# A depool, cross-projection and channel-mix chain: two projections as plain float32 matmuls, and the first loads in another order

## The chip, the cores and the metric

The kernel runs on one core of a Trainium2 chip. The metric is the device time of one execution in microseconds. Five engines work side by side, each through its own queue of instructions in order: TensorE (PE, matmuls and transposes through the array, results into PSUM), VectorE (DVE), ScalarE (ACT), GpSimd (POOL) and SyncE (SP, which here only issues transfers). PEld is TensorE's loading of the stationary operand.

## What is computed

There are 16 batches of 512 rows with 512 channels (`x`), a context of 512 rows with 1024 channels per batch, and a table of patch lengths. Cut to what matters, for each batch:

```python
n1   = layernorm(x)
h    = rmsnorm(n1) * g_res @ W_in + b_in               # "a"
hp   = rmsnorm(ctx) * g_init                           # first 512 channels are used
s[t] = ADEC * s[t-1] + BCOEF * hp[t]                   # scan over the 512 rows
x    = x + h + s[plug]                                 # plug: rows from a running sum of patch lengths
n2   = layernorm(x);  prev = n2 shifted down by one row
xk   = mu_k * n2 + (1 - mu_k) * prev                   # xr the same with mu_r
k    = square(relu(xk @ W_k.T))                        # "k"
x    = x + sigmoid(xr @ W_r.T) * (k @ W_v.T)           # "r", "v"
```

All of it is float32, with four projections of 512x512x512 per batch: a, k, r and v.

## The kernel before

**Matmuls in three passes.** A float32 operand is split into a high part (rounded to the matmul's reduced float32 type, `F32R`) and a low part (the rest). A projection of 512 columns and one block of 128 rows is twelve matmuls of 128x128x512: high by high, high by low weights, low by high weights, each over four pieces of the 512 channels (`QW`, line 595). The split takes, for each of four pieces, a cast on ScalarE (high) and a subtraction on VectorE or GpSimd (low). This holds for the weights (`hi_w`, `lo_w`, lines 574 and 577, into `wha`, `wla` and so on), for x (`split_x`, line 638, into `xh`), for the mixes (`mix`, line 860, into `m`) and for k (`k_mm`, line 904, into `ka`). A plain float32 matmul is used only for `pm` (line 1114, a mean of the weights under g_res, from which the correction of the weights, line 1124, is worked out) and for the scan's carry `pc` in the first two batches (line 749).

**One batch.** Context rows are squared and summed on ScalarE (`sq`), scaled and scanned over four interleaved row blocks on VectorE (`scan_u`), carried over the partitions by one matmul (`scan`), updated and written to a scratch tensor in memory (`dr`). Meanwhile x is turned by TensorE for the batches in `BY_PE` (`turn_x`, results `tx`; other batches load a transposed copy, `raw`), split, and projected (`a_first` for batch 0, `a_mm` for the others, results `pa`). The bias is added to x either by VectorE or GpSimd (batches in `BIAS_ADD`) or by an accumulating transfer issued by GpSimd (line 703). `a_end` (line 809) adds the projection, scaled by the row's inverse deviation, to x on VectorE. Four gathers from `dr` accumulate into x (`gather`, line 816, indirect transfers of GpSimd; for b < `NLATE` after the row ends). `norm2` normalizes (result `y`, on VectorE for batches in `Y_DVE`, else on ScalarE), `transp` turns y (`tr`), `mix` makes the two shifted mixes, and k, r and v follow, then stores. `a_first` and `k_first` go through the channel pieces in the outer loop and the four row blocks in the inner one, so all four results end together; `a_mm` finishes one row block after the other.

**Order.** Every piece of work is registered with a cost, its reads and writes, and a due time (`Plan.add`). `Plan.order` (line 119) plays the engines and transfers through and fixes each engine's queue by earliest deadline among what is ready and has a free buffer. Due times of matmuls come from a list, `slot` (line 1069): first what `START` names (line 446: x0, a0, a1, x1, x2, a2, k0, t0), from `T0` on; then for each batch i what `PERIOD` names (line 319: projection i+1, k of i), r and v of i, with the transposes of i+1 among them. `SHIFT` moves the deadlines of a stage, `ONLY` (line 392) pins the subtractions and bias adds of a stage to VectorE (0) or GpSimd (1), `ON_ACT` and `KR_DVE` choose engines for row statistics and squares. All queues are fixed when the program is built. `WARM` (line 419) puts dummy matmuls of 128x128 ahead of some groups, `HEAT` dummy matmuls of 512 columns at the very start.

**First loads.** Line 1094 on: the small constants, W_in (`load_w("a")`, two halves, tiles `wsa`), the scan's constants, the four row blocks of x0; then line 1134 on: g_init broadcast, the four context blocks of batch 0, b_in broadcast. Deadlines `at` fix this order in SyncE's queue.

Of the kernel before, what the change touches and what calls it, by code (L numbers as in the profile page):

```python
# [26 lines left out]
NC = 4  # L27
# [262 lines left out]
class InOrder:  # L290
# [27 lines left out]
PASS = 0.935  # L318
PERIOD = lambda i: (("a", i + 1), ("k", i))
TAT = {0: (0, 1), 2: (2, 3)}  # L320
TAT_OF = {0: {0: (0, 1, 2, 3)}, 1: {0: (0, 1, 2, 3)}, 2: {0: (0, 1, 2, 3)}}
# [3 lines left out]
HEAT = 8  # L325
SHIFT = {
    ("a", 0): 2.1,
    ("gather", 0): 23.8,
    ("k", 0): 2.0,
    ("load", 0): -10.1,  # L330
    ("mix_k", 0): 5.2,
    ("mix_r", 0): -10.7,
    ("norm2", 0): -17.9,
    ("plugs", 0): -30.6,
    ("rv", 0): 1.3,
    ("scan", 0): -7.2,
    ("sq", 0): -19.5,
    ("stat1", 0): -7.7,
    ("store", 0): 1.6,
    ("wk", 0): -5.2,  # L340
    ("wv", 0): -6.2,
    ("a", 1): 10.4,
    ("bias", 1): 2.6,
    ("gather", 1): 3.0,
    ("k", 1): 4.0,
    ("mix_k", 1): -1.5,
    ("mix_r", 1): -3.9,
    ("norm2", 1): -3.6,
    ("plugs", 1): 0.3,
    ("rv", 1): 12.6,  # L350
    ("split_x", 1): -7.5,
    ("sq", 1): -9.3,
    ("stat1", 1): 0.2,
    ("a", 2): 1.0,
    ("bias", 2): 53.6,
    ("gather", 2): -18.5,
    ("load", 2): 5.1,
    ("mix_k", 2): 1.2,
    ("mix_r", 2): 4.1,
    ("norm2", 2): 6.6,  # L360
    ("rv", 2): -0.4,
    ("scan", 2): 0.4,
    ("split_x", 2): -5.3,
    ("sq", 2): 30.1,
    ("stat1", 2): -1.6,
    ("store", 2): -50.4,
    ("a", 3): 8.2,
    ("bias", 3): -12.0,
    ("gather", 3): -1.8,
    ("k", 3): -3.2,  # L370
    ("load", 3): -3.1,
    ("mix_r", 3): -1.7,
    ("norm2", 3): 10.1,
    ("split_x", 3): 9.0,
    ("sq", 3): 2.7,
    ("stat1", 3): -16.2,
    ("store", 3): 9.3,
    ("a", 4): 13.9,
    ("bias", 4): -18.4,
    ("gather", 4): 11.9,  # L380
    ("k", 4): 4.9,
    ("load", 4): 16.5,
    ("mix_k", 4): 0.0,
    ("mix_r", 4): -47.3,
    ("norm2", 4): -4.5,
    ("plugs", 4): 4.7,
    ("rv", 4): -2.0,
    ("split_x", 4): -0.3,
    ("sq", 4): 2.2,
    ("stat1", 4): 2.5,  # L390
    ("store", 4): -10.4,
}
ONLY = {
    ("rv", 0): 0,
    ("k", 2): 0,
    ("wr", 0): 0,
    ("k", 3): 1,
    ("mix_r", 0): 0,
    ("split_x", 3): 0,
    ("bias", 1): 0,  # L400
    ("wk", 0): 1,
    ("mix_r", 2): 0,
    ("rv", 3): 0,
    ("mix_k", 0): 1,
    ("wv", 0): 0,
    ("wv", 1): 0,
    ("mix_k", 3): 1,
    ("rv", 2): 0,
    ("wk", 3): 1,
    ("bias", 3): 0,  # L410
    ("wr", 2): 0,
    ("wr", 3): 1,
    ("mix_k", 2): 1,
    ("split_x", 2): 0,
    ("wv", 2): 0,
}
BIAS_ADD = (0, 1)
BY_PE = (0, 1, 2)
WARM = {
    ("k", 1, 0): 1,  # L420
    ("x", 2): 32,
    ("a", 3, 0): 15,
    ("r", 0, 0): 14,
    ("a", 2, 1): 7,
    ("a", 0, 0): 29,
    ("x", 0): 1,
    ("v", 0, 0): 10,
    ("x", 1): 1,
}
TIE = 5.0  # L430
KR_DVE = (1, 3, 4, 5, 10, 11, 15)
# [4 lines left out]
RAW_IN = {2: ("op", "raw")}  # L436
CX_IN = {}
NLATE = 4
NWHOLE = 2
Y_DVE = (0, 1, 2, 3)  # L440
LEAD = 12.0
HI_DVE = False
U_DVE = True
LOADS = ["raw2"]
B_DUE, P_DUE = 3.31, 83.3
START = [("x", 0), ("a", 0), ("a", 1), ("x", 1), ("x", 2), ("a", 2), ("k", 0), ("t", 0)]
T0 = 14.3
ON_ACT = (0, 1, 3, 4, 5, 6, 9, 10, 11, 13, 15)
# [3 lines left out]
def block_kernel(  # L452
# [88 lines left out]
    LO = ((DVE, 0.61), (POOL, 1.26))  # L541

# [94 lines left out]

    def split_x(b, c):
        if b in BY_PE:
            n, t = f"xh{b}_{c}", f"tx{b}_{c}"  # L640
            add((ACT, 0.52), lambda e: e.copy(S[n][:, 0], S[t]), K(t, *J), K(n, 0), new={n: OP}, early=40)
            add((DVE, 0.6), lambda e: e.tensor_tensor(S[n][:, 1], S[t], S[n][:, 0].bitcast(F32), ALU.subtract),
                K(t, *J) + K(n, 0), K(n, 1))
            return
# [99 lines left out]
    def scan(b):  # L744
# [3 lines left out]
        if b < NWHOLE:  # L748
            add((PE, 1.12), carry, K(f"cx{b}_{NJ - 1}") + K("consts"), K(f"pc{b}"),
                new={f"pc{b}": PST if b == 0 else PS}, lead=LEAD if b > 1 else 0.0)  # L750
        else:
# [10 lines left out]
            def carry3(e):  # L762
# [4 lines left out]
                new={f"pc{b}": PS}, lead=LEAD if b > 1 else 0.0)  # L767
# [13 lines left out]

    def a_mm(b, j, due, kind=PS):
        n = f"pa{b}_{j}"
        sl = slice(j * P, (j + 1) * P)
        new = warm(("a", b, j), {n: kind}, due)
        for k, (q, w) in enumerate(QW):
# [8 lines left out]
    def a_first():  # L795

        ns = [f"pa0_{j}" for j in J]
        new = warm(("a", 0, 0), {n: TRP for n in ns}, due["a", 0, 0])
        for k, (q, w) in enumerate(QW):
# [274 lines left out]
    for what, b in START:  # L1074
        if b < NB and (what != "x" or b in BY_PE):
            for j in J:
                slot((what, b, j), 0.43 if what in "tx" else 3 * PASS)
# [16 lines left out]
    add((SP, 0.5), lambda e: e.dma_start(small_in, small_d), (), K("cols") + K("msk") + K("tri"), moves=0.45, at=-9.5)  # L1094
    load_w("a", at=-9)
    add((SP, 0.5), lambda e: e.dma_start(consts, consts_d), (), K("consts"), moves=0.4, at=-8.5)
    for j in J:
        load_x0(j, -8)
# [32 lines left out]
    def row(src, dst, k, at):  # L1131
        add((SP, 0.5), lambda e: e.dma_start(dst, src.unsqueeze(0).broadcast_to([P, D])), (), K(k), moves=0.8, at=at)

    row(ginit[0:D], g_bc, "g_bc", -6.4)
    for j in J:
        load_ctx(0, j, at=-6)
# [14 lines left out]
    def prepare_batch(b):  # L1151
# [50 lines left out]
        if b == 0:  # L1202
            a_first()
# [128 lines left out]
```

## Time and profile before

Times of three runs: 812.93, 815.05 and 817.34 us, median 815.05. One execution was profiled:

| | us |
|---|---|
| the profiled execution's own time | 813.32 |
| its span, first to last instruction | 811.2 |
| first matmul of projection a, batch 0 | 18.66 |
| first row ends of batch 0 on VectorE | 34.93 |
| first transposes of y, batch 0 | 54.96 |
| first matmul of k, batch 0 | 70.04 |
| first matmul of r, batch 0 (dummies ahead of it from 82.54) | 83.29 |
| matmul busy time, whole span | 789.8 |
| VectorE busy time, 0 to 82.5 us | 71.4 |
| ScalarE busy time, 0 to 82.5 us | 53.4 |
| GpSimd busy time, 0 to 82.5 us | 41.4 |

The time of an execution is a little more than its span. Busy times count overlapping ends of pipelined matmuls once. All instructions but a few are recorded under one line of a helper (L300), so groups are told apart by the names of their tiles: `pa`, `pk`, `pr`, `pw` are the results of a, k, r, v; `tx` and `tr` the transposes of x and y; `pm` and `pc` the two float32 matmuls; `wsa` the unsplit weights, `wha` and `wla` their parts, and likewise with k, r and v.

### The profile page before, as it was taken

To read this page: it belongs to the slowest core of one execution; us is meant where nothing else is said; L and a number is where in the kernel's file an instruction comes from. 1 tells how busy PE (TensorE), PEld (TensorE's weight loads), DVE (VectorE), ACT (ScalarE), POOL (GpSimd) and SP (SyncE) were. 2 spreads that over 40 slices of the span, in tenths; PEclk is the share of its full clock that TensorE was granted. 3 is DMA by queue.
4 is the path that set the end of the run, shared out by engine and by line. 5 is a ranking of instruction groups with operands and counts; after the bars stand their busy time and mean duration, and the time that the engine had idled before them with its cause. 6 is when DMAs were issued, how large, how long until landed. Compare 5 with 4: busy or idle time off the path is not lost.

```text
span 811.2 us, 11218 instructions
## 1 busy us (share of the span) xinstructions
PE 789.8 (97%) x3627; PEld 624.8 (77%) x3627; DVE 616.2 (76%) x1323; ACT 486.7 (60%) x950; POOL 449.8 (55%) x374
## 2 busy tenths in 40 slices
PE   7998999999999999999999999999999999999997
PEld 4776777877777887878787887888778787888885
DVE  6899799989789497686968779685876869784622
ACT  5937496555484566757455775646666564655640
POOL 2843676464675465763647566565665647571300
PEclk9999999999999999999999999999999999999999
DMA  9857486884784773847668392866559477350001
GB/s 321 271 96 263 101 235 175 280 216 131 157 232 131 181 232 74 241 166 198 156 140 242 74 268 107 218 198 184 135 130 246 136 173 216 66 141 2 27 27 52
DMA packets 52554, 134.69 MB, mean 166 GB/s; under 512 B 4752, under 2 KB 5264, under 8 KB 50576
## 3 DMA queue, kind: packets, MB, share of 16 engines
q1 hardware_dynamic: 35744, 102.39, 36.9%
q0 software_dynamic: 16608, 31.46, 23.0%
q8 instruction: 28, 0.46, 0.2%
q14 instruction: 30, 0.25, 0.1%
q10 hardware_dynamic: 144, 0.13, 0.0%
HBM read 85.73 MB, written 33.55 MB: 147 GB/s over the span
## 4 chain that ended last, share of the span: by engine, by line
PE 62%; DVE 12%; DMA 9%; POOL 6%; issue 5%; ACT 4%; SPq 0%; POOLq 0%; DVEq 0%; ACTq 0%
PE pk L300 19%; PE pr L300 15%; PE pw L300 14%; PE pa L300 11%; DMA x<-dr,plug 6%; DVE cx L300 4%; PE tr L300 3%; DVE pv L300 2%; DVE x L300 2%; POOL m L300 2%; DMA dr<-cx 2%; POOL x L300 2%; ACT pv L300 2%; PE pc L300 1%; ACT junk L300 1%
## 5 line engine op out<-in xcount | busy, mean ns | idle before, releaser
L300 POOL TENSOR_TENSOR m<-pv,m 128x512 fp32r<-128x512 f32 x79 | 117.1, 1492 | 54.6 <-ACT m L300 23.3
L300 PE MATMUL pr<-whr,m 128*128 128x512 f32 x512 | 141.7, 400 | 0.8 <-ACT sg L300 0.8
L300 PE MATMUL pa<-wha,xh 128*128 128x512 f32 x512 | 136.0, 400 | 5.6 <-DVE x L300 2.7
L300 POOL DMA_INDIRECT x<-dr,plug x64 | 109.8, 1715 | 55.8 <-DMA dr<-cx 16.8
L300 PE MATMUL pw<-whv,ka 128*128 128x512 f32 x512 | 138.9, 397 | 0.6 <-ACT sg L300 0.6
L300 PE MATMUL pk<-m,whk 128*128 128x512 f32 x512 | 134.4, 397 | 2.5 <-DVE x L300 2.1
L300 ACT ACTIVATE pv<-tr,om 128x384 f32<-128x384 f32 (+1 forms) x256 | 100.5, 488 | 57.7 <-PE tr L300 44.6
L300 PEld LDWEIGHTS pa<-wha,xh 128*128 128x128 f32 x512 | 94.8, 188 | 33.4 <-DVE x L300 7.3
L300 PEld LDWEIGHTS pk<-m,whk 128*128 128x128 f32 x512 | 95.2, 188 | 27.9 <-DVE x L300 2.9
L300 PEld LDWEIGHTS pw<-whv,ka 128*128 128x128 f32 x512 | 95.6, 188 | 24.1 <-ACT sg L300 1.8
L300 PEld LDWEIGHTS pr<-whr,m 128*128 128x128 f32 x512 | 94.0, 188 | 22.3 <-ACT sg L300 1.2
L300 DVE SCALAR_TENSOR_TENSOR pv<-tr,small,pv 128x511 f32<-128x511 f32 x128 | 95.0, 743 | 11.3 <-ACT pv L300 9.2
L300 ACT ACTIVATE y<-x,r 128x512 f32<-128x512 f32 x48 | 39.0, 816 | 97.3 <-DVE r L300 95.3
L300 DVE TENSOR_TENSOR sg<-pw,sg 128x512 f32<-128x512 f32 (+1 forms) x65 | 44.0, 678 | 55.6 <-PE pw L300 55.4
L300 POOL TENSOR_TENSOR xh<-raw,xh 128x512 fp32r<-128x512 f32 x48 | 64.4, 1348 | 39.1 <-ACT xh L300 22.6
L300 POOL TENSOR_TENSOR x<-x,sg 128x512 f32<-128x512 f32 x14 | 19.3, 1378 | 113.9 <-DVE sg L300 94.5
L300 ACT CAST m<-pv 128x512 fp32r<-128x512 f32 x128 | 73.2, 628 | 15.1 <-DVE pv L300 12.2
L300 ACT ACTIVATE junk<-cx 128x1024 bf16<-128x1024 f32 x64 | 67.9, 1061 | 12.3 <-DMA cx<-cx 11.6
L300 ACT ACTIVATE sg<-pr 128x512 f32<-128x512 f32 x64 | 38.1, 598 | 56.5 <-PE pr L300 47.3
L300 PE MATMUL pa<-wla,xh 128*128 128x512 f32 x256 | 70.4, 398 | 0.3 <-POOL wla L300 0.3
L300 PE MATMUL pw<-wlv,ka 128*128 128x512 f32 x256 | 70.7, 398 | 0.0
L300 PE MATMUL pr<-wlr,m 128*128 128x512 f32 x256 | 70.3, 396 | 0.0
(116 smaller groups left out, 1300.7 us busy)
## 6 DMA issues: line engine op xcount, KB each, us to landing
cx<-cx SPq DMA_DIRECT2D x64, 512.0 KB, 6.2
dr<-cx SPq DMA_DIRECT2D x64, 256.0 KB, 3.4
out<-x SPq DMA_DIRECT2D x31, 512.0 KB, 2.8
x<-x SPq DMA_DIRECT2D x15, 1024.0 KB, 4.9
x<-bc POOLq DMA_DIRECT2D x14, 1024.0 KB, 8.1
raw<-xT SPq DMA_DIRECT2D x26, 512.0 KB, 7.5
wsa<-winT SPq DMA_DIRECT2D x2, 512.0 KB, 4.4
x<-x SPq DMA_DIRECT2D x4, 256.0 KB, 7.0
```

The lines of the kernel that those rows point to most:

```text
L300: r = self._tc.keep_in_program_order(op(*args, **kwargs))
```

## The change

Projection a of batches 0 and 1 (`A_WHOLE`) takes four float32 matmuls per row block, on the unsplit weights `wsa` and on an unsplit copy `xt` of the transposed x, which ScalarE or VectorE copies from PSUM. The split weights of a are still made, for the batches from 2 on. Batch 0's projection goes row block by row block (`ROWS_FIRST`). The projection of batch 2 and the transposes of x2 leave `START`, so they come in the period of batch 1, ahead of its k and behind r and v of batch 0. The first loads follow a list, `FIRST`: context first, then W_in and x0. `WARM` is empty. Engine choices change: y of batches 0 and 1 on ScalarE, the low parts of wr and wv on GpSimd, batch 0's bias on GpSimd, batch 1's bias by transfer and batch 2's on GpSimd, other squares and statistics; batch 3 gathers ahead of its row ends (`NLATE`). All deadlines shift (`SHIFT`), and with them each engine's order. The carry's `LEAD` gets a second constant for late batches.

```diff
+WHOLE = 0.86
-TAT = {0: (0, 1), 2: (2, 3)}
-TAT_OF = {0: {0: (0, 1, 2, 3)}, 1: {0: (0, 1, 2, 3)}, 2: {0: (0, 1, 2, 3)}}
+TAT = {2: (0, 1, 2, 3)}
+TAT_OF = {0: {0: (0, 1, 2, 3)}, 1: {3: (0, 1), 5: (2, 3)}, 2: {2: (0, 1), 4: (2, 3)}, 3: {0: (0, 1), 2: (2, 3)}, 4: {0: (0, 1), 2: (2, 3)}}
-HEAT = 8
+HEAT = 9
...
-    ("split_x", 2): 0,
-    ("wv", 2): 0,
+    ("wr", 1): 1,
+    ("rv", 1): 0,
+    ("bias", 1): 1,
+    ("split_x", 2): 1,
 }
-BIAS_ADD = (0, 1)
+BIAS_ADD = (0, 2)
 BY_PE = (0, 1, 2)
-WARM = {
-    ("k", 1, 0): 1,
-    ("x", 2): 32,
-    ("a", 3, 0): 15,
-    ("r", 0, 0): 14,
-    ("a", 2, 1): 7,
-    ("a", 0, 0): 29,
-    ("x", 0): 1,
-    ("v", 0, 0): 10,
-    ("x", 1): 1,
-}
+WARM = {}
...
-RAW_IN = {2: ("op", "raw")}
-CX_IN = {}
-NLATE = 4
+RAW_IN = {0: ("op", "raw"), 1: ("op", "raw"), 3: ("raw", "op")}
+CX_IN = {1: ("cx", "op"), 2: ("op", "cx"), 3: ("op", "cx")}
+NLATE = 3
 NWHOLE = 2
-Y_DVE = (0, 1, 2, 3)
+FIRST = ["cx0_3", "small", "cx0_0", "consts", "g", "cx0_1", "cx0_2", "wa", "x0", "b"]
+ROWS_FIRST = True
+Y_DVE = (2, 3)
+A_WHOLE = (0, 1)
...
-LOADS = ["raw2"]
-B_DUE, P_DUE = 3.31, 83.3
-START = [("x", 0), ("a", 0), ("a", 1), ("x", 1), ("x", 2), ("a", 2), ("k", 0), ("t", 0)]
-T0 = 14.3
+LOADS = ["cx1", "raw2", "raw1"]
+B_DUE, P_DUE = 1.31, 0.91
+START = [("x", 0), ("a", 0), ("x", 1), ("a", 1), ("k", 0), ("t", 0)]
+T0 = 1.55
...
+    CP = ((ACT, 0.52), (DVE, 0.6))
...
+    def xt(b, c):
+
+        return S[f"xt{b}_{c // 2}" if b in BY_PE else f"raw{b}_{c // 2}"][:, c % 2]
+
     def split_x(b, c):
+        if b in A_WHOLE:
+            if b in BY_PE:
+                n, t = f"xt{b}_{c // 2}", f"tx{b}_{c}"
+                add(CP, lambda e: copy(e, S[n][:, c % 2], S[t]), K(t, *J) + (K(n, "a") if c % 2 else []),
+                    K(n, c % 2) + ([] if c % 2 else K(n, "a")), new=None if c % 2 else {n: STAGE}, early=40)
+            return
...
     def a_mm(b, j, due, kind=PS):
         n = f"pa{b}_{j}"
         sl = slice(j * P, (j + 1) * P)
         new = warm(("a", b, j), {n: kind}, due)
+        if b in A_WHOLE:
+            for c in range(NC):
+                add((PE, WHOLE), lambda e, c=c: e.matmul(S[n], xt(b, c)[:, sl], st("a", c), start=(c == 0), stop=(c == NC - 1)),
+                    XT(b, c) + K(f"wsa{c // 2}", c % 2), K(n), new=None if c else new, due=due + c * WHOLE, early=AHEAD)
+            return
...
-                slot((what, b, j), 0.43 if what in "tx" else 3 * PASS)
+                slot((what, b, j), 0.43 if what in "tx" else 4 * WHOLE if what == "a" and b in A_WHOLE else 3 * PASS)
...
+    for k, what in enumerate(FIRST):
+        load_first(what, 0.05 * k - 9.5)
...
-        if b == 0:
+        if b == 0 and not ROWS_FIRST:
             a_first()
         for j in J:
-            if b:
-                a_mm(b, j, due["a", b, j], PST if b == 1 else PS)
+            if b or ROWS_FIRST:
+                a_mm(b, j, due["a", b, j], PST if b < 2 else PS)
             a_end(b, j)
```

## The prediction

> **What bounds the kernel now.** I read the busy table first, then the busy tenths, the stretches of the first 83 us, TensorE's timeline and last SyncE's queue. The first view gives share of the span and instruction counts.
>
> ```profile
> PE 789.8 (97%) x3627; PEld 624.8 (77%) x3627; DVE 616.2 (76%) x1323; ACT 486.7 (60%) x950; POOL 449.8 (55%) x374
> ...
> PE   7998999999999999999999999999999999999997
> ```
>
> TensorE is the bound nearly everywhere; the waits that release it after 82.5 us add up to 4.3 us in all. So the span is: the moment at which the first k is through, plus the rest of TensorE's work, plus a tail (its last matmul ends near 806.3 us, the span at 811.2 us). The stretches show where the beginning differs (columns: stretch, length, then busy time and count of PE, PEld, DVE, ACT, POOL, granted clock, DMA share, GB/s).
>
> ```profile
> 15.00:16.00 1.00, 1.00 (x12) 1.00 (x11) 0.97 (x4) 1.00 (x3) 0.07 (x1) 0.50 1.04 412
> ...
> 20.00:40.00 20.00, 18.05 (x113) 14.10 (x114) 17.63 (x39) 18.30 (x44) 16.99 (x15) 1.00 0.81 277
> 40.00:60.00 20.00, 18.40 (x93) 14.68 (x92) 19.21 (x51) 6.42 (x15) 10.28 (x11) 1.00 0.63 101
> 60.00:80.00 20.00, 17.14 (x80) 12.16 (x79) 19.76 (x44) 16.37 (x34) 6.94 (x6) 1.00 0.77 264
> ```
>
> From 40 to 80 us VectorE is busy 19 to 20 us of 20, TensorE is not: up to the first k the bound is VectorE and the chain through it. TensorE's timeline (start, us, engine, line, op, result<-operands, count, and in brackets what it waited for) gives the prices.
>
> ```profile
> 5.29 3.67 PE L300 MATMUL pm<-wsa,gmean 128*128 128x512 f32 x8
> 9.52 2.58 PE L300 MATMUL tx<-consts,x 128*128 128x128 f32 x16 [0.56 <-DMA x<-x]
> ...
> 14.78 3.27 PE L300 MATMUL pa<-ones 128*128 128x128 f16 x29 [0.50 <-DVE pf L300]
> 18.66 1.20 PE L300 MATMUL pa<-wha,xh 128*128 128x512 f32 x4 [0.61 <-ACT wha L300]
> ...
> 33.30 1.91 PE L300 MATMUL tx<-consts,x 128*128 128x128 f32 x16
> ...
> 70.04 2.46 PE L300 MATMUL pk<-m,whk 128*128 128x512 f32 x8 [0.74 <-DVE x L300]
> ...
> 82.54 0.94 PE L300 MATMUL pr<-ones 128*128 128x128 f16 x14
> 83.29 1.17 PE L300 MATMUL pr<-whr,m 128*128 128x512 f32 x4
> 84.30 1.09 PE L300 MATMUL pr<-wlr,m 128*128 128x512 f32 x4
> 85.23 2.03 PE L300 MATMUL pr<-whr,m 128*128 128x512 f32 x8
> 87.10 1.10 PE L300 MATMUL pr<-wlr,m 128*128 128x512 f32 x4
> ```
>
> The last rows: eight split matmuls from 85.23 to 87.10, 0.234 us each, so 2.80 us for one row block's twelve and 11.2 us for a projection. The first row: four float32 matmuls, two records each, whose weight loads start 0.43 us apart: 0.86 us for one float32 matmul, and the carry matmul at 62.28 us (next weights but one at 63.14) agrees. Sixteen transposes of x take 1.7 us. The first k ends at 82.5 us.
>
> **Cost, part by part.** *Float32 projections.* Four matmuls of 0.86 replace twelve of 0.234: 3.44 against 2.80 us a row block, +0.64 x 8 = +5.1 us of TensorE; a projection is 13.8 us. This comes from rows, so it has no bounds to speak of.
>
> *Placeholders.* All dummy matmuls go. Behind the first k they stand at 82.54 (0.75 us), 88.03 (0.55), 104.39 (0.04) and 141.99 (0.82): -2.2 us. Those before it lay mostly in idle time. One more heat matmul, 0.43 us, lies where TensorE waits for loads.
>
> *Third projection.* Its 11.2 us and its 1.7 us of transposes move from before the first k to behind v of batch 0. They cost the same there; what they covered is the chain of batch 0 from projection to k. Batch 1's own chain now has k, r and v of batch 0 and this projection as cover, about 46 us. So the remainder after the first k is 811.2 - 82.5 = 728.7, - 2.2 + 11.2 + 1.7 = 739.4 us. The break-even end of the first k is 811.2 - 739.4 = 71.8 us.
>
> *VectorE.* Gone or moved before the first k: 12 low parts of x at 0.68 (8.2), batch 2's four row ends at 0.74 (3.0), y of batch 0 at 0.54 (2.2, now ScalarE, plus 0.6 of small ones), six bias adds at 0.69 (4.1), eight low parts of wr and wv at 0.65 (5.2, now GpSimd at 1.3 each, 10.4 us). That is 22 of the 71.4 us VectorE was busy up to 82.5. GpSimd had 41.4 us of those 82.5, so it can carry it; if wr or wv come late there, r waits and each microsecond counts in full. Batch 1's bias becomes an accumulating DMA (2.0 us of GpSimd's queue and 8.8 us to landing), batch 2's the opposite; cover is k of batch 0.
>
> *First loads.* The same ten items in another order. SyncE's queue in the order now:
>
> ```profile
> 0.72 0.39 SPq L300 DMA_DIRECT2D small<-small_d  x1
> 1.17 0.93 SPq L300 DMA_DIRECT2D wsa<-winT  x2
> 2.14 0.47 SPq L300 DMA_DIRECT2D consts<-consts_d  x1
> 2.65 1.85 SPq L300 DMA_DIRECT2D x<-x  x4
> 4.55 0.56 SPq L300 DMA_DIRECT2D bc<-ginit  x1
> 5.17 4.61 SPq L300 DMA_DIRECT2D cx<-cx  x4
> ```
>
> Landing times (issue plus time to landing): wsa 6.4, x 9.3 to 11.4, cx 13.4 to 17.0, b 17.9 us. I read the new order off the same cumulated bytes: cx0_0 6.4, cx0_1 10.3, cx0_2 12.0, wsa 13.4 and 14.5, x 15.2 to 17.0, b 17.9 us. The projection's loads are 6 to 8 us later, the scan's some 5 to 7 us earlier. The wait this adds is pm's on wsa; behind it on TensorE stand the transposes of x0 and all of a0, and for those wait the row ends on VectorE and the gathers on GpSimd.
>
> *First projection's start.* The g correction waits for pm, so pm starts at 13.4 instead of 5.3 us, after 8 us with hardly a matmul. Estimate: 13.4 + 3.44 + 1.65 for half clock (in the stretch at 15 us it was 0.50, and the 29 dummies ran 3.27 us, half of which is lost) = 18.5. Then 1.7 for transposes, 0.6 for a copy from PSUM (no split) and some hops: 21.0 us. Bounds: 18.3 (x landed at 17.0, last transpose, copy; pm at full clock) and 25.3 (first rival).
>
> *Up to k.* 21.0 + 13.8 = 34.8; x1's transposes and a1, + 1.7 + 13.8 = 50.3. Batch 0's rows now end one by one from 24.5 us, the scan's rows are stored by about 24 (15 us carry, four updates at 0.62, 3.6 to landing), so gathers run under a1: last row end 35.5, gather 1.7 + 5.0, statistics and y about 3.5: ready near 46. In due order a1 comes first, then t0: + 1.7 = 52.0. From t0 to the first k matmul lie one shifted copy 0.74, one mix 0.95, one cast 0.63 and hops, 2.5 us, unless t0 slips between a1's groups as tr did between a2's at 54.96. Ends 0 and 2.5; I take 1.2, between them, next to the 0.74 us that k waited at 70.04. k starts at 53.2 and ends after 11.2 + 0.4 for the counts at 64.8 us.
>
> *Clock.* TensorE stood still from about 12.2 to 14.1 us, short of 3 us, and the stretches after it show 0.50. By this row a wait of 2 us before k could cost 1.65 us more. But the 2.02 us wait at 66.24 was followed by full clock, so I add nothing; by the first row the time would be 809.7. The Trainium skill (TensorE: Matmul & The Clock Gate, "Why this matters for your kernels") speaks against taking warm-up matmuls away, and allows gaps up to about 3 us between bursts. An estimate by that page is my sum unchanged, 808.0: the 8 us gap ahead of pm is charged, the one ahead of k is not. The 2 us gap at 12.2 us, followed by half clock, differs from the page.
>
> *Order anew, the rest of the run.* Shifts, engine choices, the gather of batch 3 ahead of its row ends. Bounds from the waits of 4.3 us behind the first k: none left, -4.3, or twice as much, +4.3. I take 0, as VectorE keeps a quarter of each 48 us batch free.
>
> **Sum.** 64.8 + 739.4 = 804.2 against 811.2: -7.0 us. The profiled execution took 813.3, 2.1 more than its span, and lies 1.7 under the median 815.05; I put the difference on the median: **808.0 us**. From 811.0 to 819.1 us is within 0.5%.
>
> **Rivals.** *First: the weight correction queues on VectorE.* The four corrections of wsa waited behind other work now: pm ended at 8.96, the last correction at 19.08, 10.1 us later. If so again, it ends at 28.6, row 0 ends 5.0 us later than above, and the time is 813.0, no change. For it: scan, copies and corrections meet on VectorE between 14 and 21 us. Against: now nothing else waited for the corrections at once, the loads of x being late.
>
> *Second, the slower side: batch 0's chain is no shorter.* From the row ends at 34.93 us to k at 70.04 it took 35.1 us, with VectorE full. Again 35.1 after 34.8 gives k at 69.9, through at 81.5, 9.7 beyond break-even: 815.05 + 9.7 = 824.8 us. It decides against the change when k begins later than 64.3 us. For it: the cover of a2 is gone. Against: 22 us less on VectorE, and rows that end one by one.
>
> *Third: the new order leaks later.* Doubled waits behind k, +4.3: 812.3, no change; a gather or load one batch late would show as repeated waits.
>
> *Fourth: no gap and full clock.* a0 at 18.3, k at 18.3 + 29.3 + 1.7 = 49.3, through at 60.9: 804.1; with the later waits gone as well, 799.8.
>
> **Chances.** Forecast 0.48, fourth 0.17, first 0.12, third 0.08, second 0.15. Range 800 (fourth with no waits) to 818 (a third of the second's price beyond break-even). Faster 0.65 (forecast and fourth), within 0.5% 0.21 (first, third and 0.01 for a second that comes in part), slower 0.14. Half a per cent is about what a measurement of this kernel can tell from no change.
>
> **What would show it.** Right: pm after 13 us, the first a0 matmul at 19 to 23, eight rows of 3.44 us, first k matmul at 50 to 56, r at 62 to 68, and from there 739 us to the end. Wrong: corrections of wsa spread over 10 us; k later than 60; VectorE full from 25 to 60; r waiting for wlr on GpSimd; waits of over 0.4 us a batch later.

## The result, and the profile after

The changed kernel took 819.16 us (median of 19 runs, 815.79 to 823.0), the kernel before 813.67 us (19 runs, 811.71 to 817.34). The ratio is 1.0068, with a 95% interval from 1.0057 to 1.0080: 5.5 us slower, where 7 us faster was forecast. The profiled execution took 821.07 us, 1.9 above its median, with a span of 819.3 us against 811.2.

First the busy table and TensorE's tenths of the changed kernel (engine, busy us, share of the span, instructions).

```profile
PE 788.1 (96%) x3486; PEld 615.4 (75%) x3486; DVE 604.6 (74%) x1299; ACT 490.4 (60%) x954; POOL 472.0 (58%) x391
...
PE   4977999999999999999999999999999999999997
```

TensorE's work is all but the same (788.1 against 789.8 us), and from the fifth slice of 20.5 us on it is as full as before. Only the first slices differ. The stretches of the changed kernel show where (columns as in the prediction).

```profile
20.00:40.00 20.00, 19.11 (x68) 9.77 (x67) 16.13 (x44) 16.80 (x37) 13.99 (x13) 1.00 0.86 261
40.00:60.00 20.00, 15.69 (x39) 6.95 (x37) 14.35 (x35) 12.47 (x22) 14.08 (x13) 0.91 1.00 282
60.00:80.00 20.00, 15.81 (x80) 11.42 (x79) 16.50 (x39) 15.19 (x36) 9.14 (x8) 1.00 0.64 238
```

From 40 to 60 us TensorE was busy 15.69 us instead of 18.40, VectorE 14.35 instead of 19.21. So VectorE was not the bound; both waited. The transfer engines were full (share 1.00, 282 GB/s) in a stretch in which they moved 101 GB/s at 0.63 before. TensorE's timeline of the changed kernel gives each step of the prediction its measured moment.

```profile
15.01 6.44 PE L300 MATMUL pm<-wsa,gmean 128*128 128x512 f32 x8 [8.08 <-DMA wsa<-winT]
21.29 1.91 PE L300 MATMUL tx<-consts,x 128*128 128x128 f32 x16
...
24.00 2.82 PE L300 MATMUL pa<-wsa,xt 128*128 128x512 f32 x6
...
27.74 11.40 PE L300 MATMUL pa<-wsa,xt 128*128 128x512 f32 x26
38.98 1.91 PE L300 MATMUL tx<-consts,x 128*128 128x128 f32 x16
41.40 5.42 PE L300 MATMUL pa<-wsa,xt 128*128 128x512 f32 x12 [0.51 <-ACT xt L300]
50.62 1.38 PE L300 MATMUL pc<-cx,consts 128*128 128x512 f32 x2 [3.81 <-issue]
51.79 10.20 PE L300 MATMUL pa<-wsa,xt 128*128 128x512 f32 x20
61.84 1.91 PE L300 MATMUL tr<-consts,y 128*128 128x128 f32 x16
66.31 3.07 PE L300 MATMUL pk<-m,whk 128*128 128x512 f32 x12 [2.56 <-ACT m L300]
70.05 1.20 PE L300 MATMUL pk<-m,whk 128*128 128x512 f32 x4 [0.67 <-ACT m L300]
...
81.47 1.20 PE L300 MATMUL pr<-whr,m 128*128 128x512 f32 x4 [1.00 <-ACT kr L300]
```

To be seen: `pm` waits 8.08 us for W_in and then needs 6.3 us up to the first transposes. The first projection starts at 24.00 us. In the second one, TensorE stops for 3.81 us after twelve of its 32 records, and what stands there is not the projection but `pc`, the carry of batch 1's scan. The profile names no releaser for this stop ("issue"); in e2, below, the same stop (4.41 us) is put down to VectorE's `cx`. The twenty records behind it take 10.05 us instead of 8.6. k starts at 66.31 us, r at 81.47. The last row but one shows k stopping again for its mixes.

What held the carry is in VectorE's timeline of the changed kernel.

```profile
47.98 0.69 DVE L300 BATCH_NORM_STATS2 sb<-x 128x6 f32<-128x512 f32 x1 [3.36 <-DMA x<-dr,plug]
...
49.11 1.41 DVE L300 SCALAR_TENSOR_TENSOR cx<-cx,cx 128x512 f32<-128x512 f32 x2
...
52.17 1.28 DVE L300 SCALAR_TENSOR_TENSOR cx<-pc,cx 128x512 f32<-128x512 f32 x2
...
57.99 2.23 DVE L300 SCALAR_TENSOR_TENSOR x<-pa,rs,x 128x512 f32<-128x512 f32 x3 [1.49 <-DMA x<-bc]
```

The first row is a row statistic of batch 0 that waits 3.36 us for a gather. Behind it in VectorE's queue stand the scan steps of batch 1 (second row) on which the carry depends, although their own operands were there. The carry stops TensorE, and the rest of projection a of batch 1 stands behind the carry. The last row: the row ends of batch 1, which also wait, for the accumulating transfer of the bias. The late gather is the third, issued by GpSimd at 37.63 us. Its row among the transfers of the changed kernel (KB left out for indirect ones; the last number is us from issue to landing) and the loads beside it in SyncE's queue:

```profile
x<-dr,plug POOLq DMA_INDIRECT x1, 10.3
```

```profile
30.59 7.27 SPq L300 DMA_DIRECT2D wsr<-wrT  x2
37.91 0.56 SPq L300 DMA_DIRECT2D cx<-cx  x1
38.57 5.82 SPq L300 DMA_DIRECT2D wsv<-wvT  x2
```

It took 10.3 us from issue to landing, the fourth 8.8, the first two 6.5 and 5.2. The loads of W_r, of batch 2's context and of W_v were issued just ahead of it and beside it.

### The profile page after: what moved, and what is told of

Same layout as the page of the kernel before. It is cut to its first block, busy times and chain, and to the rows that moved or that the text cites. A ratio compares the mean times of both kernels' runs of the same rounds, so it can differ in the third digit from the quotient of the medians.

```text
span 819.3 us, 10896 instructions
## 1 busy us (share of the span) xinstructions
PE 788.1 (96%) x3486; PEld 615.4 (75%) x3486; DVE 604.6 (74%) x1299; ACT 490.4 (60%) x954; POOL 472.0 (58%) x391
## 4 chain that ended last, share of the span: by engine, by line
PE 64%; DMA 3%; ACT 3%; DVE 2%; POOL 2%; issue 1%; SPq 0%; POOLq 0%; DVEq 0%
PE pk L300 18%; PE pa L300 16%; PE pr L300 14%; PE pw L300 13%; DMA dr<-cx 3%; DVE cx L300 2%; ACT pv L300 1%; PE tr L300 1%; POOL m L300 1%; PE pc L300 1%; ACT junk L300 1%; POOL x L300 1%; DMA cx<-cx 1%; DVE sg L300 0%; ACT sg L300 0%
## 5 line engine op out<-in xcount | busy, mean ns | idle before, releaser
L300 POOL TENSOR_TENSOR m<-pv,m 128x512 fp32r<-128x512 f32 x81 | 120.9, 1541 | 48.7 <-DVE m L300 15.1
L300 POOL DMA_INDIRECT x<-dr,plug x64 | 108.8, 1700 | 57.0 <-issue 13.3
L300 PE MATMUL pr<-whr,m 128*128 128x512 f32 x512 | 139.4, 399 | 1.9 <-ACT kr L300 1.0
L300 PE MATMUL pa<-wha,xh 128*128 128x512 f32 x448 | 118.2, 397 | 0.0
L300 ACT ACTIVATE y<-x,r 128x512 f32<-128x512 f32 x56 | 45.4, 815 | 99.7 <-issue 51.1
L300 PEld LDWEIGHTS pa<-wha,xh 128*128 128x128 f32 x448 | 83.7, 188 | 21.1 <-DVE x L300 1.5
L300 POOL TENSOR_TENSOR xh<-raw,xh 128x512 fp32r<-128x512 f32 x51 | 71.5, 1416 | 35.6 <-ACT xh L300 15.2
L300 POOL TENSOR_TENSOR x<-x,sg 128x512 f32<-128x512 f32 x18 | 23.7, 1318 | 117.9 <-DVE sg L300 109.2
L300 PE MATMUL pk<-m,wlk 128*128 128x512 f32 x256 | 69.6, 395 | 0.0
```

The costliest lines, as they stand in the source:

```text
L300: r = self._tc.keep_in_program_order(op(*args, **kwargs))
```

## The experiments

In all of them the span is taken apart at two points of TensorE's timeline: the first matmul of k and the first of r of batch 0. What follows r is nearly the same in all relatives of the changed kernel, so r's start decides. Each ratio is to the kernel before as timed beside that run (its median lay between 813.57 and 814.61 us). For a span of 811.2 us with the changed kernel's remainder of 819.3 - 81.47 = 737.8 us, r would have to start at 73.4 us.

| kernel | ratio to before, 95% interval | k starts | k to r | r starts | span - r |
|---|---|---|---|---|---|
| before | 1 | 70.0 | 13.3 | 83.3 | 727.9 |
| changed | 1.0068 (1.0057 to 1.0080) | 66.3 | 15.2 | 81.5 | 737.8 |
| p1_float32_alone | 1.0019 (0.9999 to 1.0039) | 68.6 | 13.6 | 82.1 | 732.8 |
| p2_loads_alone | 1.0042 (1.0020 to 1.0064) | 74.5 | 13.7 | 88.2 | 730.6 |
| u2_third_back | 1.0233 (1.0192 to 1.0273) | 83.4 | 14.1 | 97.5 | 730.3 |
| e1_scan_first | 1.0014 (0.9998 to 1.0030) | 62.4 | 15.7 | 78.1 | 735.8 |
| e2_clock_pm | 1.0051 (1.0030 to 1.0071) | 65.0 | 15.2 | 80.2 | 736.0 |
| e3_both | 1.0010 (0.9998 to 1.0022) | 62.3 | 15.9 | 78.2 | 736.0 |
| e4_hold_loads | 1.0016 (1.0000 to 1.0031) | 61.5 | 15.2 | 76.6 | 737.5 |
| e7_stops_removed | 1.0038 (1.0022 to 1.0055) | 58.5 | 20.1 | 78.6 | 739.7 |
| e9_scan_first_and_hold | 1.0033 (1.0020 to 1.0046) | 64.3 | 16.4 | 80.7 | 737.8 |
| e10_bias_on_gpsimd | 1.0158 (1.0135 to 1.0182) | 69.5 | 14.9 | 84.4 | 742.4 |
| e11_act_cleared | 1.0057 (1.0037 to 1.0076) | 58.2 | 18.7 | 77.0 | 739.2 |

The moments come from one profiled execution each, and the start alone varies: `pm` began at 15.01, 14.79 and 13.46 us in the changed kernel, e1 and e4, which are the same up to there, so a difference of a microsecond between two moments may be the start's. The execution of e9 took 820.35 us, 4.2 above its median; the others lie within 2.2 us of theirs but for u2, 4.1 below.

Four experiments (e1 to e4) ask what the stop in the second projection costs and who causes it. Then p1, p2 and u2 do or undo one part of the change, and e7, e9, e10 and e11 try to take all known stops away together. Numbers in a queue are pieces of work of the plan; the queues of the changed kernel were held fixed but for the move named.

### e1: batch 1's scan ahead of the waiting statistics

VectorE's queue alone is changed: the scan pieces of batch 1 come in front of the row statistics that wait for the gathers.

```diff
 VectorE's queue
+  scan 1: cx<-cx,cx x2 (209, 211), behind r0_0's piece 143
+  scan 1: cx<-pc,cx x4 (213, 215, 217, 219), behind 141
   norm2 0: sb<-x of rows 2 and 3 (147, 151)
-  scan 1: cx<-cx,cx x2
-  scan 1: cx<-pc,cx x4
```

> The changed kernel with six of VectorE's pieces moved: the last two steps of batch 1's scan go ahead of the wait for batch 0's third gather, and the four updates behind the carry as well. Nothing else changes order. Theory A (the carry matmul of batch 1 stands in the middle of projection a of batch 1 on TensorE, and its operand stood on VectorE behind a gather that landed late): TensorE's wait of 3.8 us at 46.8 us goes, and with it about 1.4 us of half clock; a1 ends near 56 instead of 61.9, k of batch 0 begins near 60.5 instead of 66.3, and the time falls by 5 to 6 us, to about 813.5 (ratio to the kernel before about 1.000). Rival B (the chain of batch 0 through gathers, norm and mixes is what k waits for): a1 ends earlier but k still begins at 64 to 66, time 817 to 819. Rival C (what comes behind k binds, the squares, counts and weights of r): k begins earlier, r does not, 818 to 819.

It took 815.92 us. TensorE's timeline of this kernel:

```profile
45.94 1.02 PE L300 MATMUL pc<-cx,consts 128*128 128x512 f32 x2
...
62.42 6.00 PE L300 MATMUL pk<-m,whk 128*128 128x512 f32 x16 [5.13 <-ACT m L300]
...
78.11 1.20 PE L300 MATMUL pr<-whr,m 128*128 128x512 f32 x4 [1.73 <-ACT kr L300]
```

The carry at 45.94 us waits for nothing, y of batch 0 is turned 6.5 us earlier (55.38 against 61.84), though the gathers took as long as before (10.6 and 9.4 us for the third and fourth). Of the 6.5 us, 0.9 lie in that execution's earlier start (first projection at 23.13 us). So the stop was an order of two things in one queue, and it is worth 3 to 4 us (3.2 between the medians, 0.54% between the ratios), where theory A had 5 to 6. But a new wait of 5.13 us stands in front of k, and behind it the granted clock was 0.63 from 62.4 to 68.4 us: k's first sixteen matmuls take 5.83 us, the next sixteen 3.73. VectorE's timeline of the same kernel names what the wait hangs on:

```profile
58.15 2.73 DVE L300 SCALAR_TENSOR_TENSOR x<-pa,rs,x 128x512 f32<-128x512 f32 x4 [2.80 <-DMA x<-bc]
60.79 0.74 DVE L300 SCALAR_TENSOR_TENSOR pv<-tr,small,pv 128x511 f32<-128x511 f32 x1
```

The row ends of batch 1 wait 2.80 us for the bias transfer, and k's shifted copies (second row) stand behind them. Of 6.5 us gained at the transposes, 3.9 are left at k and 3.4 at r.

### e2 and e3: the clock of the first matmuls

A hundred dummy matmuls of 128x128 fill the wait ahead of `pm`; e3 adds e1's order.

```diff
+        def mean_of(e, c=c):
+            if c == 0:
+                for _ in range(100):
+                    e.matmul(S["pm"][:, :P], ones, ones, start=True, stop=True)
-        add((PE, PASS), lambda e, c=c: e.matmul(S["pm"], ...
+        add((PE, PASS), mean_of,
```

> The changed kernel with 100 dummy matmuls of 128x128 on TensorE between the batch counts (6.9 us) and the first wsa matmul (15.0 us), which lie in idle time. Theory D (half clock after the removed warm-up cost the start 2.8 us: pm took 6.3 us for 3.44): pm ends near 18.5, projection a of batch 0 begins near 21.3 instead of 24.0, and if nothing else binds the end moves by 2 to 3 us, to about 816.5. Rival: the stop in projection a of batch 1 ends when the gather of batch 0 lands, whose time the loads set; then the gain is lost there, 818.5 to 819.5.

> Both of the edits, VectorE's pieces moved and the dummies ahead of pm. If A and D hold and add up: k begins near 58, time about 811 (ratio 0.997). If B holds, k begins no earlier than 62, time 815 or more.

TensorE's timeline of e2:

```profile
7.60 7.38 PE L300 MATMUL pm<-ones 128*128 128x128 f16 x100 [0.81 <-DVE cum L300]
14.82 3.65 PE L300 MATMUL pm<-wsa,gmean 128*128 128x512 f32 x8
...
65.04 5.55 PE L300 MATMUL pk<-m,whk 128*128 128x512 f32 x16 [2.56 <-ACT m L300]
70.43 3.90 PE L300 MATMUL pk<-m,wlk 128*128 128x512 f32 x16
```

`pm` now needs 3.5 us up to the transposes at 18.31, 2.8 less than in the changed kernel, so its slowness came of the wait ahead of it. The first projection starts only 1.1 us earlier (22.93): it now waits 0.90 us for a copy of the turned x on ScalarE, which the slow `pm` had hidden. The stop in the second projection is still there, and 1.3 us is left at r. e2 took 817.95 us, e3 815.18: neither against the changed kernel nor on top of e1 do the dummies give anything that can be told apart (the ratios' intervals overlap). The last two rows of e2 come back in the last section.

### e4: who makes the gathers late

The changed kernel's own order; SyncE issues batch 2's first context block, and with it W_v behind it in its queue, only when the last gather of batch 0 has landed (138 is that gather, 278 that load).

```diff
+        if p.n == 138:
+            gathered = last.name
+        if p.n == 278:
+            tc.add_manual_dep(last, gathered, AFTER, ...)
```

> The changed kernel in its own order; only, SyncE's queue waits ahead of the context of batch 2 and of W_v until the last gather of batch 0 has landed. Theory E (the gather landed late because it shared the transfer engines with those loads: 10.3 and 8.8 us from issue to landing, against 4.5 to 6.8 in the kernel before): the third gather lands at 44 to 45 instead of 47.9, the carry follows near 47 instead of 50.6, and the time falls by 3 to 5 us, to 814 to 816. Rival (the gathers are slow by themselves, or because of the loads issued before, those of W_r): third gather lands as before, time 818 to 820 or more, since the held loads are then late for r and v.

It took 815.86 us. The third gather among the transfers of this kernel:

```profile
x<-dr,plug POOLq DMA_INDIRECT x1, 6.7
```

6.7 us against 10.3, the fourth 5.2 against 8.8. The carry of batch 1 then waits 0.37 us instead of 3.81, with VectorE's order as it was. So the gathers were late because of those loads, and the stop has two causes that are both needed: a late gather, and work queued behind it. How the loads hold a gather up is not shown; a full transfer engine is not enough, since the changed kernel's first two gathers landed in 6.5 and 5.2 us with a share of 0.99 (32 to 36 us). Again something takes its place, in ScalarE's timeline of this kernel:

```profile
52.42 1.06 ACT L300 ACTIVATE junk<-cx 128x1024 bf16<-128x1024 f32 x1 [7.45 <-DMA cx<-cx]
...
54.80 1.14 ACT L300 CAST whv<-wsv 128x512 fp32r<-128x512 f32 x2 [0.53 <-DMA wsv<-wvT]
```

The square of batch 2's context waits 7.45 us for the load that was held back, and y of batch 0 and k's mixes are behind it. k starts 4.8 us earlier than in the changed kernel, of which 1.7 lie in the earlier start of this execution, and its first sixteen matmuls take 6.15 us (granted clock 0.60 from 61.5 to 67.8 us).

### p1 and p2: one part of the change alone

Both are the kernel before with one part and its own constants; the queues are planned anew.

```diff
 p1_float32_alone
+A_WHOLE = (0, 1)
+ROWS_FIRST = True
 p2_loads_alone
+FIRST = ["cx0_3", "small", "cx0_0", "consts", "g", "cx0_1", "cx0_2", "wa", "x0", "b"]
```

> The kernel before with the first part of the change alone: projections of batches 0 and 1 as float32 matmuls, row block by row block; loads, place of the third projection, warm-up dummies, shifts and engine choices as before. Theory G (up to k of batch 0 VectorE and the chain bind, so the 5.1 us that TensorE pays more are covered, and 8 low parts less on VectorE help): 811 to 814, same as before or up to 3 us better, k of batch 0 at 67 to 70. Rival (the 5.1 us are paid): 818 to 820, that is, as slow as the changed kernel, and the float32 matmuls would be the cause.

> The kernel before with the order of the first loads alone: context first, then W_in and x0. Theory (projection a of batch 0 begins some 4 to 6 us later, but three projections stand between it and k, and the chain through VectorE sets k's begin): k begins at 69 to 72, time 813 to 816. Rival (a later start is paid in full, since TensorE's work before k is what counts): k at 74 or later, 817 to 820.

p1 took 817.01 us, between the two expected ranges, with a ratio that can just be no change at all. k starts 1.5 us earlier and r 1.2 us earlier, although TensorE has 5.1 us more to do ahead of them. So the dearer matmuls are covered there; behind r 4.9 us are lost, 3.5 of them in waits (7.8 us behind 82 us, 4.3 before); why the newly planned queues wait there is not shown. p2 took 819.03 us, with k at 74.45, as its rival had it. TensorE's timeline of p2:

```profile
14.55 3.75 PE L300 MATMUL pm<-wsa,gmean 128*128 128x512 f32 x4 [7.86 <-DMA wsa<-winT]
...
24.57 2.69 PE L300 MATMUL pa<-ones 128*128 128x128 f16 x29 [2.48 <-DVE xh L300]
27.02 4.71 PE L300 MATMUL pa<-wha,xh 128*128 128x512 f32 x16
...
74.45 1.06 PE L300 MATMUL pk<-m,whk 128*128 128x512 f32 x2
```

`pm` is 9.3 us later than before and slow, the first real matmul of the projection 8.4 us later (27.02 against 18.66), k 4.4 us. About half of the late start is made good by k; that the scan's earlier loads do it is not shown. r is 4.9 us late, and 2.7 more are lost behind it. The two parts add up to 0.61%, close to the 0.68% of the whole change. The rest of it, the third projection's place and the new order, is then worth about nothing; that is a sum over runs and was not shown by itself. The equal size says little, too: p1 loses its time behind r, where the changed kernel kept to its sum.

### u2: the third projection back in its place

```diff
-START = [("x", 0), ("a", 0), ("x", 1), ("a", 1), ("k", 0), ("t", 0)]
+START = [("x", 0), ("a", 0), ("x", 1), ("a", 1), ("x", 2), ("a", 2), ("k", 0), ("t", 0)]
```

> The changed kernel with the third projection back in front of the first k (order planned anew with the other constants of the change). Theory H (the third projection was cover: moving it away left TensorE idle while batch 0's chain ran, so that what the move saves is lost as idle time): TensorE's waits between a1 and k shrink from 2.6 + 3.8 us to under 2, the first k ends at 88 or earlier, and the time is no worse than the changed kernel's, 814 to 819. Rival (the move itself gains, and its place was right): first k ends later than 90, 821 or more.

It took 833.67 us. k starts 17.1 us later than in the changed kernel, and only 7.5 us come back behind r, where 11.2 + 1.7 were to be expected. The queues were planned anew with deadlines that had not been made for this order: batch 2's projection stands wholly ahead of batch 0's transposes (at 77.81 us) instead of between them and k, the first projection starts 2.9 us later, and the second stops 3.10 us for a statistic. So the run says that this program is bad, and not whether the third projection's place is.

### e7, e9, e10, e11: all stops at once

e7 is the changed kernel with e2's dummies, e4's hold, and, on ScalarE, the squares of batch 2's context and the casts of W_v moved in among k's mixes.

```diff
 ScalarE's queue
-  sq 2 (295, 296) and wv 0 (183 to 189) among batch 0's y
+  wv 0 (183 to 189) behind the cast of k's third mix (383), sq 2 (295, 296) behind the fourth (387)
```

> The changed kernel with three stops taken away at once: dummy matmuls ahead of pm, loads of the context of batch 2 and of W_v held until batch 0's last gather has landed, and on ScalarE the squares of batch 2's context and the casts of W_v moved behind the mixes of k (with the loads held they stood, with a wait of 7.5 us, ahead of y of batch 0). Theory A+E (the change lost in the first 80 us through queues that stop behind transfers, and nowhere else): k of batch 0 begins near 58 to 59 instead of 66.3, r near 71 to 72 instead of 81.5, and the time is 811 to 813, no slower than the kernel before. Rival F (PSUM: the four results of a1 must be ended before k can have its banks, and they wait for the accumulating bias transfer, so k can't begin before about 59.5): 813 to 815. Rival C (squares of k and weights of v bind): 815 or more.

It took 818.05 us. k does start at 58.5, as it should, but r takes 20.1 us from there: k's matmuls wait 2.6, 1.0 and 1.5 us for mixes on ScalarE, which now come late for the casts among them.

e9 joins e1's order, the dummies and the hold.

> The changed kernel with the scan steps of batch 1 moved ahead on VectorE (as in the run scan first), the dummies ahead of pm, and the loads held until the last gather of batch 0 landed (as in the run hold loads). Theory one, single stops: each of the two known stops has its own cause. Gathers land in about 6 us, the carry of batch 1 comes before 46 us without a wait, and the accumulating transfer of the bias, no longer beside loads, lands in 8 to 10 us instead of 13, near 54. Then VectorE's row ends of batch 1 don't stand in front of k's mixes for more than 1 us: k begins at 57 to 59 us, r at 72 to 74, span 809 to 811, ratio to the kernel before 0.994 to 0.998. Theory two, what is freed is lost at the next wait: k no earlier than 61 us, r at 76 to 78, span 813 to 815, ratio 1.000 to 1.003.

It took 816.18 us. The two stops are gone: the carry starts at 45.26 us without a wait, and the row ends of batch 1 wait 0.60 us for the bias. But k starts at 64.28. ScalarE's timeline of this kernel:

```profile
55.47 1.14 ACT L300 CAST whv<-wsv 128x512 fp32r<-128x512 f32 x2 [2.94 <-DMA wsv<-wvT]
...
59.35 1.14 ACT L300 CAST whv<-wsv 128x512 fp32r<-128x512 f32 x2 [2.02 <-DMA wsv<-wvT]
...
61.45 2.28 ACT L300 ACTIVATE pv<-tr,om 128x384 f32<-128x384 f32 x6
```

The casts of W_v wait 2.94 and 2.02 us for the held load, in front of the last y (56.52) and of the first mix of k (third row).

e10 is e9 with batch 1's bias added on GpSimd instead, and batch 2's by transfer; SyncE's queue was planned anew, with the held loads behind the last gather.

```diff
-BIAS_ADD = (0, 2)
+BIAS_ADD = (0, 1)
```

> As the run scan first and hold, but the bias of batch 1 is added by four GpSimd instructions behind the last gather of batch 0, instead of by the accumulating transfer (batch 2's by the transfer instead); the loads of the next context and of W_v are put behind the last gather in SyncE's order, too. Theory one, single stops: the wait of VectorE's row ends of batch 1 for the transfer (2.8 us, and 5.1 us of k's mixes behind it) is gone, and no other of its size stands there: k begins at 56 to 58 us, r at 71 to 73, span 808 to 811, ratio 0.993 to 0.998. Theory two, what is freed is lost at the next wait: r at 76 to 78, span 813 to 816, ratio 1.000 to 1.004; the new wait is then for GpSimd's low parts of wr, which stand behind the adds, or for the mixes themselves.

It took 827.36 us. The four adds occupy GpSimd from 43.41 for 6.28 us, the first inverse deviations of batch 0's rows stand behind them (49.66 instead of 41.78 in e9), the second projection waits 2.90 us for a copy and then runs its first twelve records in 8.24 us, and 4.6 us more are lost behind r. With this much changed at once the run doesn't price the bias transfer; it only shows that GpSimd had no room for the adds there.

e11 is e9 with ScalarE cleared: the casts of W_v and the squares of batch 2 behind the last mix of r, batch 2's row statistics behind k's squares, and their followers on VectorE and GpSimd likewise.

```diff
 ScalarE's queue
-  wv 0 (183 to 189), sq 2 (296) among batch 0's y
   mix_k 0, mix_r 0 (to 431)
+  wv 0 (183 to 189), sq 2 (295 was left, 296 to 298)
   k 0 (401 to 415)
+  stat1 2 (321 to 328)
```

> As the run scan first and hold, with what stood in ScalarE's queue ahead of batch 0's y and of k's mixes moved behind them: the casts of W_v and the squares of batch 2's context behind the last mix of r, batch 2's row statistics behind the squares of batch 0's k (their followers on VectorE, and the low parts of W_v on GpSimd, likewise). Theory one, single stops in queues: the waits of 2.9 and 2.0 us of ScalarE for the held load of W_v no longer stand ahead of the last y and the mixes, so k, which began at 64.3 us there, begins at 56 to 59 us, takes 13 to 15 us to r (70 to 73 us), and the span is 807 to 811 us, ratio to the kernel before 0.992 to 0.998. Theory two, what is freed is lost at the next wait: k before 60 us, but r at 75 us or later (k's mixes, counts or kr late, or the low parts of r's mixes), span 813 to 818, ratio 1.000 to 1.005.

It took 819.16 us. TensorE's timeline of e11:

```profile
58.24 1.77 PE L300 MATMUL pk<-m,whk 128*128 128x512 f32 x4 [2.56 <-ACT m L300]
60.76 5.36 PE L300 MATMUL pk<-m,whk 128*128 128x512 f32 x12 [0.75 <-ACT m L300]
...
73.09 0.25 PE L300 MATMUL cp<-ohj,oh 128*128 128x4 f16 x4 [1.08 <-DVE sq L300]
...
76.94 0.16 PE L300 MATMUL cp<-bm,small 128*128 128x3 f16 x1 [1.63 <-DVE bm L300]
76.96 1.17 PE L300 MATMUL pr<-whr,m 128*128 128x512 f32 x4
```

k starts at 58.24 us, as it should, and r takes 18.7 us from there. The first theory is right in its first half and wrong in its second, as the second had it: k stops 2.56 and 0.75 us for its mixes, runs at a lower clock behind that (see the last section), and waits 1.08 us for the masks (the row names `sq`, which stands right behind them) and 1.63 for the sums of the next patch lengths. The masks took VectorE 4.71 us, beside GpSimd's subtractions, and the sums stand in VectorE's queue behind pieces that wait 1.03 us for the squares that I had moved. In no run did r start before 76.6 us. No version beat the kernel before; the nearest, e3, is at 1.0010 (0.9998 to 1.0022).

## Why the prediction was wrong

**The failed step is "Up to k".** Its sum from the start of the first projection to r was 64.8 - 21.0 = 43.8 us; measured were 57.5. In its order:

- *a0, 13.8 us:* 15.0, with 0.89 us of wait for the patch counts. The price of a float32 matmul was right: its records stand 0.43 us apart in the full rows.
- *x1's transposes and a1, 1.7 + 13.8 us:* 2.4 and 20.4. This is the largest miss, and it is a mechanism and not a size. I took the projection as 32 records in a row and put what stands among them at nothing, without a look. What stands there is batch 1's carry (1.2 us), and with it TensorE's queue hung on VectorE's, and VectorE's on a gather: 3.81 us of stop, and 1.45 us more for the records behind it (granted clock 0.66 from 52 to 56 us). e1 and e4 show both links, each removing the stop from one side. The clock term, which I had put at nothing for the wait ahead of k, was nothing there in this execution; it came behind this stop.
- *Gather 1.7 + 5.0 us:* the first two kept to it (6.5 and 5.2 to landing), the third and fourth took 10.3 and 8.8. The duration came from a stretch with the transfer engines at 0.63; the change put the loads of a context block and of W_v beside the later gathers (e4). The rows did not end one by one from 24.5 us either: the first piece of all four went in front, the first row ended from 31.53 us on, the last from 40.14 (35.5 in the sum).
- *Batch 1's bias, "cover is k of batch 0":* wrong. Its row ends stand on VectorE ahead of k's mixes, and the transfer needed 13.1 us to land, not 8.8. In the changed kernel it cost 1.49 us of VectorE, hidden by the later stop; e1, where it comes last, shows 2.80.
- *From transposes to k, 1.2 us:* 2.56, the upper end of the bounds that I had given (2.5), as ScalarE had the mixes' first halves to do.
- *k in 11.2 + 0.4 us:* 15.2, at full clock. TensorE stops 0.67 us for a mix, 0.92 for a mask and 1.00 for squares. I priced k's matmuls and not the mixes, casts and counts that now run beside k. In the kernel before, p1 and p2 groups of projection 2 stand between the transposes and k, and k to r takes 13.3 to 13.7 us; where projection 2 comes behind r, it takes 14.9 to 20.1, in the experiments partly for a lower clock (see below).

**The start was mis-sized.** 24.00 us against 21.0 and within its bounds: `pm` started 1.6 us later than my sum of bytes said, and took 6.3 us, not 5.1, as it ran at about half speed all the way and not for a part. The 1.6 us are one execution's: in the changed kernel and the nine runs made from it, `pm` began between 13.43 and 15.01 us. My list of what VectorE saves adds up to 23.3 us, not 22; no term of the sum rests on it.

**The rest was right.** From r to the end it took 737.8 us against the 739.4 of the sum. Waits behind 82 us are 4.8 us in all, against 4.3 before, so the third rival didn't come.

**The rivals.** The second, the slower side, gave its deciding point rightly: k later than 64.3 us, and it began at 66.31. Its mechanism did not come. The chain from the end of the first projection to k took 27.3 us, not 35.1, and VectorE was idle for 5.7 of the 20 us from 40 on; the loss is in order and waits, not in work. The first rival came in part: the corrections of W_in ended at 29.6 us, 8.3 after `pm`, but cost little, since matmuls of all four rows on the first piece of W_in filled the time. The fourth did not come: the start was 24.00 us, not 18.3.

The errors add up: 3.0 at the start, 1.2 in a0, 0.7 at x1, 6.6 in a1, 1.6 up to k and 3.6 in k are 16.7 us, and r did start 16.7 us late. Less 1.6 in the remainder, the span is 15.1 us longer than forecast. The time is 11.2 us longer (819.16 against 808.0): the profiled execution lies 1.9 above its median, and the one that the forecast starts from 1.7 under.

**Why clearing the stops did not save it.** e7, e9 and e11 bring the transposes to 54 us and k to 58.2 at best, and r still starts at 77 or later. One part is the clock behind the wait in front of k, which no expectation had. Sixteen of k's matmuls take 3.73 us at full clock (e1, 68.25 to 71.98 us); its first sixteen, behind waits of 2.56 to 6.24 us, took 5.4 to 6.6 us in e1, e2, e3, e4, e9 and e10, with a granted clock of 0.55 to 0.72. Without these 1.7 to 2.9 us, k to r would be 12.2 to 13.6 us there, no longer than in the kernel before. That is an estimate from the rows, not a run. So the wait in front of k cost more than its length, and in the kernel before, projection 2 had filled most of that time.

The other part is the work that had gone on under projection 2 (mixes, casts of W_r and W_v, squares of the next context). It stood ahead of k's mixes (e4, e9), among them (e7) or behind them (e11), and TensorE waited for it or for the mixes each time, in front of k or inside it. That every order must end so is not shown. What remains open is how much of this a plan made anew for this order could hide, since the moves here were made by hand in fixed queues; and what the third projection's place is worth alone, since u2 doesn't show it.

## What to carry to other kernels

When a stretch of matmuls is priced, list what else stands in TensorE's queue inside it, and for each such instruction follow the queue it hangs on to its head: one late transfer behind two in-order queues stopped a projection that had all its operands. A duration of a transfer holds for the transfers that were beside it in the stretch that it was read from; if the change moves loads there, look for a row with such loads beside it (here 8.8 to 10.3 us against 5.2 to 6.7). And cover that is moved away is to be priced by the work that it covered on every engine, not only by the wait that the trace shows, because after one wait is removed the next in-order queue shows its own. A wait of TensorE can also cost more than its length, through the clock behind it.

## What the hardware showed

**A gather beside loads.** The four gathers of batch 0 took 6.5, 5.2, 10.3 and 8.8 us to land in the changed kernel and 6.5, 5.4, 6.7 and 5.2 in e4, where loads were held, with GpSimd's queue in the same order. The accumulating transfer beside the same loads took 13.1 us, against a median of 8.3 over the run.

**The clock after a wait of 2.56 us.** In the changed kernel k began after such a wait and ran twelve matmuls in 3.07 us, at full clock (1.00 from 66 to 69 us). In e2 the wait was the same, with no second one behind it, and the granted clock was 0.72 from 65 to 71 us, with 0.50 from 67 to 69: sixteen matmuls took 5.39 us (rows of e2 above). In e11 the wait was as long, followed by one of 0.75, and the granted clock behind it was this (stretches of e11):

```profile
58.00:61.00 3.00, 2.01 (x5) 1.15 (x6) 1.56 (x4) 1.10 (x3) 0.00 (x0) 0.60 1.02 308
61.00:66.00 5.00, 5.00 (x13) 3.34 (x14) 4.77 (x10) 4.60 (x12) 0.24 (x1) 0.55 1.02 399
66.00:69.00 3.00, 3.00 (x15) 2.41 (x14) 3.00 (x6) 1.97 (x5) 2.28 (x2) 1.00 1.01 404
```

About 0.6 for some 8 us, and full from 66 on. So waits of one length ended in both ways, and what decides between them is not shown. The Trainium skill (TensorE: Matmul & The Clock Gate, "Why this matters for your kernels") advises against gaps above about 3 us between bursts of matmuls; the single gap of e2 was shorter, and half clock came behind it all the same, so here the page's figure is no safe bound. The column itself is no safe witness at the start: it stood at 1.00 from 15 to 21 us in the changed kernel while `pm`'s weight loads came 0.86 us apart, and the dummies of e2 brought `pm` from 6.3 to 3.5 us.

**VectorE beside GpSimd.** Two views of the changed kernel, VectorE's and GpSimd's timeline:

```profile
70.84 0.69 DVE L300 TENSOR_TENSOR m<-pv,m 128x512 fp32r<-128x512 f32 x1
...
72.22 1.32 DVE L300 TENSOR_TENSOR m<-pv,m 128x512 fp32r<-128x512 f32 x1
...
74.25 3.93 DVE L300 TENSOR_TENSOR oh<-hj,small 128x512 f16<-128x512 f32 x3
```

```profile
71.69 1.30 POOL L300 TENSOR_TENSOR m<-pv,m 128x512 fp32r<-128x512 f32 x1 [7.93 <-DVE m L300]
74.04 1.30 POOL L300 TENSOR_TENSOR m<-pv,m 128x512 fp32r<-128x512 f32 x1 [1.05 <-ACT m L300]
75.86 1.77 POOL L300 TENSOR_TENSOR m<-pv,m 128x512 fp32r<-128x512 f32 x1 [0.53 <-ACT m L300]
```

A subtraction of two tiles on VectorE takes 0.69 us (70.84) and 1.32 (72.22) when it begins while GpSimd's own subtraction runs (71.69 to 72.99). The three masks take 3.93 us where they took 0.65 to 0.69 each before. The Trainium skill (SBUF — State Buffer, "SBUF: two separate sides") states that a VectorE instruction with two inputs in SBUF and a GpSimd instruction that reads SBUF lock a pair of ports against each other, the later one waiting for the whole of the other; the start and length of these rows agree with it. The rows shown are of the mixes' low parts. The low parts of W_r on GpSimd, which I took for free, had a price on VectorE as well: beside them (52.84 to 55.34 us) one subtraction of W_in's low parts took 1.21 us, the other three 0.68 each. It was small, as VectorE had to wait for the bias transfer behind it.
